# A four-layer convolution network on one core: sixth position of the first 3x3 convolution in filtered form, outer column sums and a normed residual moved to ScalarE and accumulating DMAs

## The chip, the cores and the metric

The kernel runs on one core of a Trainium2 chip. The metric is the device time of one execution in microseconds (us), as the median over several runs. The core has five engines with an instruction queue each, and every queue is worked off in order: PE (TensorE, matrix products; PEld is its weight load), DVE (VectorE), ACT (ScalarE), POOL (GpSimd) and SP (SyncE, which only issues transfers). Transfers issued by POOL go through one software queue (q0 in the profile), those of SP through a hardware queue (q1). Transfers that add to their destination (`accum_op=ALU.add`) are issued by POOL throughout this kernel.

## The reference, cut to what matters

Four layers, each `x = x + layer(groupnorm(x))`, on x of shape (4, 256, 56, 56) in float32. Layers 0 and 2 are involutions, layer 3 is a gate from a Fourier transform. The change lies in layer 1 alone, two 3x3 convolutions with batch norms and a residual:

```python
def _L1_conv_ref(x, w1, g1, b1, rm1, rv1, w2, g2, b2, rm2, rv2):
    h = _conv3x3(x, w1, stride=1)
    h = jax.nn.relu(_bn(h, g1, b1, rm1, rv1))
    h = _conv3x3(h, w2, stride=1)
    h = _bn(h, g2, b2, rm2, rv2)
    return jax.nn.relu(x + h)
# --- layer 1 ---
x = x + _L1_conv_ref(_gn(x), ...)
```

So with n = groupnorm(x) the layer's output is x + relu(n + conv branch): n enters the convolution and also stands as a residual inside the relu.

## The kernel before, in words

**Stages.** `involution_layer` runs for layer 0 (to about 509 us of the span), `conv_layer` for layer 1 (to about 1208 us), and `involution_layer` again for layer 2 with layer 3 folded into it.

**Tiling of layer 1.** The 256 channels are two blocks of 128 partitions. Each of the four images is cut into three chunks of rows; the first convolution's chunks have 20, 18 and 18 rows (`C1_ROWS`), the second's 16, 20 and 20 (`C2_ROWS`). That makes 12 chunks, numbered 0 to 11, for each convolution. They alternate: conv1(0), then conv1(1), conv2(0), conv1(2), conv2(1), ... conv1(11), conv2(10), conv2(11).

**Along the rows: six positions.** A row is taken in tiles of four outputs (`WT` = 14 tiles). `transform` turns the normed input into six planes v, and each 3x3 filter row becomes six values u; an output tile comes from six products, the "positions". They are worked in the order `KS` = 1, 2, 3, 4, 0, 5. Positions 1 to 4 are combined by sums and differences on DVE, 0 and 5 are added with factors at the end (L1523 to L1536).

**Between the rows: filtered or unfiltered.** An unfiltered position (`unfiltered`, L1449) takes the three filter rows one after the other: 12 matmuls with 128x128 weights over all the chunk's rows (252 columns for 18 rows, 280 for 20). A filtered position makes two output rows from four products of sums of neighbouring rows: 16 matmuls over half the columns (126 or 140). It needs `columns(i, k, half)` (L1425): half 0, the inner sums and differences (two DVE instructions, L1434 and L1435), and half 1, the outer difference of rows two apart (one DVE instruction over the whole chunk, L1432). It also needs combined weights (`column_weights`, `filter_weights`). In conv1(i) for i > 0, five positions (`K2`) are filtered and position 5 is unfiltered; conv1(0) and all of the second convolution are unfiltered.

**A filtered position, step by step** (L1483 to L1510). PE writes two pairs of PSUM banks: `inner`, from half 0, and then `outer`, from half 1. ACT copies the first inner bank to `h` (L1502), DVE makes h + second and h - second into the rows of the position's home tile (L1506, L1507), and then adds the outer pair (L1509). PSUM holds four such pairs, so PE starts the inner pair of a position when DVE has read the inner pair of two positions before.

**The second convolution's residual.** `residual(co)` (L1554) norms the input rows `xr` on ACT into the tile `res`, of which there is one buffer for both channel blocks; `joined(co)` (L1564) adds the convolution on DVE (L1568). `added` (L1580) is then run at once for block 0 and at the start of the next chunk for block 1: relu on ACT back into xr (L1582), a POOL transfer that adds the layer's input from DRAM (L1583), and a POOL transfer of the result to DRAM (L1584). In the last chunk DVE does this itself and SP stores.

**What sets the order.** `in_order` pins each engine's instructions to program order. `conv1` and `conv2` call the lists `after[0]` to `after[11]` at fixed places between their positions, and the loop at L1674 fills these lists: the next chunk's input (`phases` on ACT, `input1` and `input2` mostly on DVE), the statistics of finished rows, loads, and the column sums of the next conv1. `FIRST` lists the column sums prepared during the conv2 before, `LATER` those made inside conv1, as their buffers (five in rotation, `new_v2`) come free. In conv1(0) and conv1(1) the second convolution's weights are built by 18 accumulating transfers on POOL (`summed_weights`, L1281), each of which waits for an earlier one.

Of the kernel before, what the change touches and what calls it, by code (L numbers as in the profile page):

```python
# [16 lines left out]
P = 128  # L17
# [55 lines left out]
def net_kernel(  # L73
# [1109 lines left out]
    def conv_layer(xin, xout, st, ahead):  # L1183
        with ExitStack() as es:
# [13 lines left out]

            KS, K2 = (1, 2, 3, 4, 0, 5), (1, 2, 3, 4, 0)
            u1_sb = wpool.tile([P, NB, 3, WPOS, C], F32, name="u1_sb")  # L1200
# [5 lines left out]
            ux0_sb = room["rows"][:, n : n + NB * C].rearrange("p (c n) -> p c n", c=NB)  # L1206

            def between_weights(ci, k0, k1):

                return ux_sb[:, ci, k0 - 1 : k1 - 1, :] if k0 else ux0_sb[:, ci : ci + 1]  # L1210

# [13 lines left out]

            n_v2, n_h = [0], [0]

            def new_v2():
                n_v2[0] += 1
                at = (n_v2[0] - 1) % 5 * NY  # L1230
                return room["v2"][:, at : at + NY]

            def new_half():
                n_h[0] += 1
                return room["v2" if n_h[0] % 2 else "xr"][:, 5 * NY : 5 * NY + NY // 2]

# [62 lines left out]
            def column_weights(ci, k0, k1):  # L1299

                w0, w1, w2 = (u1_sb[:, ci, y, k0:k1, :] for y in range(3))
                x = between_weights(ci, k0, k1)
                s = y_tile(3 if k0 else 5)[:, : (k1 - k0) * C].rearrange("p (k n) -> p k n", n=C)
                tt(s, w0, w2, ALU.add)
                tt(x, s, w1, ALU.subtract)
                tt(w1, s, w1, ALU.add)
# [118 lines left out]
            def columns(i, k, half):  # L1425

                y0, y1, _, _ = rows1(i)
                m = (y1 - y0) // 2
                v = v_of[1, i][:, VP[k]].rearrange("p (r e c) t -> p e r (c t)", e=2, c=NB)
                t = v2_of[i, k, half] = new_v2().rearrange("p (e r n) -> p e r n", e=2, n=NB * WT)  # L1430
                if half:
                    tt(t[:, :, :m], v[:, :, :m], v[:, :, 1 : m + 1], ALU.subtract)  # L1432
                else:
                    tt(t[:, 0, :m], v[:, 1, :m], v[:, 0, 1 : m + 1], ALU.add)  # L1434
                    tt(t[:, 1, :m], v[:, 0, 1 : m + 1], v[:, 1, :m], ALU.subtract)  # L1435


            FIRST = [(K2[0], 0), (K2[0], 1), (K2[1], 0), (K2[1], 1), (K2[2], 0)]
            LATER = {0: [(K2[2], 1)], 1: [(K2[3], 0), (K2[3], 1)], 2: [(K2[4], 0), (K2[4], 1)]}

# [16 lines left out]
            def conv1(i, after, tail):  # L1457
# [4 lines left out]
                a, t, b, s, q = (y_tile(k)[:, : NB * n * WT] for k in (0, 1, 2, 5, 4))  # L1462
                first = y_tile(3)[:, : NB * n * WT] if i else q
                home = {1: first, 2: s, 3: t, 4: s, 0: s}

# [14 lines left out]
                for n_s, k in enumerate(KS):  # L1480
                    if k in K2 and i > 0:
# [7 lines left out]
                        for ps, bank, v2, e, u in work4:  # L1489
                            for co in range(NB):  # L1490
                                for ci in range(NB):
                                    nc.tensor.matmul(  # L1492
                                        ps[:, bank, co * m : (co + 1) * m],
                                        u[ci][:, co * P : (co + 1) * P],
                                        v2[:, e, : n // 2, ci * WT : (ci + 1) * WT],
                                        start=(ci == 0),
                                        stop=(ci == NB - 1),
                                    )
                        for late in LATER.get(n_s, ()):
                            columns(i, *late)  # L1500
                        h = new_half()[:, : NB * m]
                        nc.scalar.copy(h, inner[:, 0, : NB * m])  # L1502
                        o = home[k].rearrange("p (r e t) -> p e r t", e=2, t=WT)
                        rows_of = lambda x: x.rearrange("p (r t) -> p r t", t=WT)
                        m2 = rows_of(inner[:, 1, : NB * m])
                        tt(o[:, 0], rows_of(h), m2, ALU.add)  # L1506
                        tt(o[:, 1], rows_of(h), m2, ALU.subtract)  # L1507
                        run_all(after[2 * n_s])
# [31 lines left out]
            def conv2(i, after, sums, tail):  # L1540
# [9 lines left out]

                res = work.tile([P, CV_ROWS * W], F32, name="res", bufs=1)[:, : n * W]

                def residual(co):

                    x = xr_of[i, co][:, : n * W]
# [8 lines left out]
                def joined(co):  # L1564

                    y = room["h"][:, : 4 * NY].rearrange("p (j n) -> p j n", j=4)[:, :, co * m : (co + 1) * m]
                    rj = res.rearrange("p (j q) -> p j q", j=4)
                    stt(rj, y, s2_6[:, co : co + 1], rj, ALU.mult, ALU.add)  # L1568
# [17 lines left out]
                def stats(co, k):  # L1586
# [3 lines left out]
                    nc.vector.bn_stats(sums[co][:, at, :], xr_of[i, co][:, r0 * W : r1 * W])  # L1590

                for n_s, k in enumerate(KS[:4]):
                    pair = two_banks()
# [48 lines left out]
            order.append((2, n_chunks - 1))  # L1642
            late_v, late_x = None, []
            sums_of = {}
# [29 lines left out]
            for s, (conv, i) in enumerate(order):  # L1674
# [5 lines left out]
                after[0] += late_x  # L1680
                late_x.clear()
                if conv == 1:
                    after[0] += tail1
                    tail1 = []

                    if nxt[0] == 2:
                        j = nxt[1]
                        late_v = input2(j)
                        place(after, late_v, (1, 1, 3, 5, 8))
                        if j == 0:  # L1690
                            place(after, weights2, (0, 1, 2, 11))
                            for ci in range(NB):
                                after[0].append(lambda ci=ci: column_weights(ci, 0, 1))
                                after[1].append(lambda ci=ci: filter_weights(ci, 0, 1))
                        if i + 1 < n_chunks:
                            place(after, phases(i + 1), range(1, 10))
                            if i + 2 < n_chunks:
                                after[9].append(lambda i=i: load_rows(i + 2, xin))
                    else:
# [9 lines left out]
                        for n, (k, half) in enumerate(FIRST):  # L1709
                            after[(8, 8, 9, 9, 10)[n]].append(lambda k=k, half=half: columns(1, k, half))  # L1710
                        for ci in range(NB):
# [3 lines left out]
                else:  # L1715
# [10 lines left out]
                    if late_v is not None:  # L1726
                        place(after, late_v, (0, 0, 1, 1))
                        late_v = None
# [7 lines left out]
                    if nxt is not None and nxt[0] == 1:  # L1736
                        j = nxt[1]
                        place(after, input1(j), (0, 0, 1, 1, 2, 3, 4, 5, 6))
                        for n, (k, half) in enumerate(FIRST):
                            after[(4, 5, 6, 7, 8)[n]].append(lambda j=j, k=k, half=half: columns(j, k, half))  # L1740
                    elif nxt is not None:
# [92 lines left out]
```

## Time and profile before

| what | us |
|---|---|
| runs, median of 3 (lowest to highest) | 1760.48 (1759.03 to 1763.52) |
| the profiled execution | 1761.49 |
| span of the profile | 1759.7 |
| PE busy in the span | 1687.6 (96%) |
| DVE / ACT / POOL busy | 1338.6 / 912.6 / 417.5 |
| layer 1, first to last matmul of L1453 and L1492 | 521.8 to 1207.4 |

Each float32 matmul stands twice in the records, so 2136 records of L1453 are 1068 matmuls. A row of the timeline gives the start, the length, the engine, the line and operation, and in brackets the idle time before it and what ended it; consecutive instructions of one kind are merged. A row of the windows gives a stretch, its length, and the busy time of PE, PEld, DVE, ACT and POOL in it (with the number of instructions), the granted TensorE clock, the busy share of the 16 DMA engines, and GB/s.

### The profile page before, as it was taken

What the parts mean: (1) busy time and instruction counts of PE and PEld (TensorE: products, weight loads), DVE (VectorE), ACT (ScalarE), POOL (GpSimd) and SP (SyncE); (2) the same over time, 40 slices, a digit from 0 to 9 for tenths busy, and PEclk for the clock granted to TensorE, in tenths of its full rate; (3) what the DMA queues carried; (4) which work ended last, traced back from release to release, by engine and by line L of the source; (5) the groups of instructions that cost most, each with busy time, mean ns of one, the idle gap of its engine ahead of it and who ended that gap; (6) DMA issues with size and microseconds to landing.
All of it is one profiled execution on the core that took longest, in us unless ns stands there. A gap on an engine that the chain in (4) does not pass through costs nothing.

```text
span 1759.7 us, 55922 instructions
## 1 busy us (share of the span) xinstructions
PE 1687.6 (96%) x24216; PEld 1494.0 (85%) x24216; DVE 1338.6 (76%) x2469; ACT 912.6 (52%) x1948; POOL 417.5 (24%) x609
## 2 busy tenths in 40 slices
PE   6999999999999999999999999998999999989998
PEld 4988988889978988898899889986988888878886
DVE  2777787777769888888889888955777678767775
ACT  2655556456546434443344334324767567557564
POOL 2223322333234000000000000001000563562572
PEclk9999999999989999999999999999999999999996
DMA  2355444533669323321333122243444666664653
GB/s 87 126 165 160 134 152 155 185 107 119 200 208 246 84 84 80 104 74 44 96 87 90 53 78 63 53 147 114 145 141 149 204 216 200 201 203 153 191 155 114
DMA packets 79876, 236.12 MB, mean 134 GB/s; under 512 B 13494, under 2 KB 29631, under 8 KB 75919
## 3 DMA queue, kind: packets, MB, share of 16 engines
q1 hardware_dynamic: 57438, 163.33, 29.4%
q0 software_dynamic: 21152, 67.95, 14.8%
q8 instruction: 191, 3.13, 0.7%
q10 hardware_dynamic: 1040, 1.26, 0.3%
q14 instruction: 55, 0.44, 0.1%
HBM read 95.07 MB, written 49.15 MB: 82 GB/s over the span
## 4 chain that ended last, share of the span: by engine, by line
PE 71%; DVE 13%; DMA 5%; ACT 4%; issue 3%; SPq 1%; POOL 1%; ACTq 0%; DVEq 0%; POOLq 0%
PE mm L1453 24%; PE ps L635 14%; PE ps L593 14%; PE mm L1492 9%; DVE kt L611 5%; PE ps L407 3%; DMA xw<-xw 3%; DVE un L655 3%; PE ps L469 2%; DMA u_sb<-in_wc_dram 1%; DVE st L1105 1%; ACT hp L488 1%; ACT xw L419 1%; PE ps L718 1%; PE ps L947 1%
## 5 line engine op out<-in xcount | busy, mean ns | idle before, releaser
L1453 PE MATMUL mm<-v,u_sb 128*128 128x280 f32 (+2 forms) x2136 | 475.6, 384 | 0.0
L1453 PEld LDWEIGHTS mm<-v,u_sb 128*128 128x128 f32 x2136 | 402.8, 189 | 67.8 <-issue 0.4
L635 PE MATMUL ps<-kt,xw 126*32 126x48 f32 (+1 forms) x12544 | 381.9, 236 | 23.0 <-issue 14.9
L635 PEld LDWEIGHTS ps<-kt,xw 126*32 126x32 f32 (+1 forms) x12544 | 344.3, 122 | 68.7 <-issue 47.3
L593 PE MATMUL ps<-hp,z_sb 64*126 64x133 f32 x6144 | 382.6, 279 | 8.1 <-DVE kt L611 4.9
L593 PEld LDWEIGHTS ps<-hp,z_sb 64*126 64x126 f32 x6144 | 363.6, 185 | 23.5 <-DVE kt L611 6.6
L611 DVE TENSOR_TENSOR kt<-ps,zb_sb 126x798 f32<-126x798 f32 x352 | 333.0, 981 | 58.8 <-PE ps L593 47.5
L604 ACT ACTIVATE kt<-ps,zb_sb 126x133 f32<-126x133 f32 x960 | 280.3, 441 | 105.9 <-PE ps L593 105.9
L655 DVE SCALAR_TENSOR_TENSOR un<-ps,s,un 128x240 f32<-128x240 f32 x224 | 102.5, 458 | 89.0 <-ACT un L650 84.9
L1492 PE MATMUL mm<-xs,u_sb 128*128 128x126 f32 (+1 forms) x1320 | 163.0, 277 | 7.0 <-DVE hp L1507 3.3
L1492 PEld LDWEIGHTS mm<-xs,u_sb 128*128 128x128 f32 x1320 | 156.3, 191 | 9.1 <-ACT ph L1361 4.0
L655 DVE SCALAR_TENSOR_TENSOR un<-ps,par_sb,un 128x240 f32<-128x240 f32 x224 | 97.8, 457 | 83.9 <-ACT un L648 79.9
L419 ACT COPY xw<-ps 126x896 f32<-126x896 f32 x112 | 101.3, 906 | 46.8 <-DMA xw<-xw 23.6
L660 POOL TENSOR_TENSOR xs<-un,xs 128x240 f32<-128x240 f32 x112 | 72.2, 665 | 218.2 <-DVE un L655 218.1
L407 PE MATMUL ps<-ident_sb,strip_sb 128*126 128x128 f32 x784 | 113.9, 286 | 9.7 <-issue 4.3
L1583 POOL DMA_DIRECT2D xs<-x x22 | 19.6, 889 | 430.6 <-ACT xs L1582 430.6
L648 ACT ACTIVATE un<-ps,par_sb 128x240 f32<-128x240 f32 x112 | 50.2, 448 | 120.8 <-PE ps L635 115.7
L650 ACT ACTIVATE un<-ps,bn_t,s 128x240 f32<-128x240 f32 x112 | 60.0, 537 | 91.3 <-PE ps L635 85.7
L1582 ACT ACTIVATE xs<-res 128x1120 f32<-128x1120 f32 (+1 forms) x22 | 46.4, 2107 | 117.0 <-DVE res L1568 117.0
L150 POOL TENSOR_TENSOR norm_sb<-norm_sb,mhalf 128x1 f32<-128x1 f32 x32 | 19.1, 598 | 368.7 <-DVE norm_sb L149 368.7
L407 PEld LDWEIGHTS ps<-ident_sb,strip_sb 128*126 128x126 f32 x784 | 86.2, 143 | 21.5 <-issue 5.8
L1361 ACT ACTIVATE ph<-xs,norm_sb 128x294 f32<-128x294 f32 (+2 forms) x96 | 78.8, 864 | 8.4 <-DMA xs<-x 6.7
(265 smaller groups left out, 1900.0 us busy)
## 6 DMA issues: line engine op xcount, KB each, us to landing
xw<-xw SPq DMA_DIRECT2D x224, 252.0 KB
xw<-xw SPq DMA_DIRECT2D x224, 126.0 KB
xs<-x SPq DMA_DIRECT2D x24, 560.0 KB
x<-xs POOLq DMA_DIRECT2D x8, 1568.0 KB, 8.1
xs<-x SPq DMA_DIRECT2D x8, 1568.0 KB
xs<-in_x_dram SPq DMA_DIRECT2D x6, 1568.0 KB
x<-xs SPq DMA_DIRECT2D x6, 1568.0 KB
gx<-x POOLq DMA_DIRECT2D x42, 224.0 KB, 5.1
```

Of the source, the lines that this page charges most:

```text
L407: nc.tensor.transpose(ps[:Q, k * P : (k + 1) * P], flat[:, k * Q : (k + 1) * Q], ident_sb)
L419: nc.scalar.copy(xw[:, :NSB, :], ps[:Q, : NSB * P].rearrange("q (n c) -> q n c", n=NSB))
L593: nc.tensor.matmul(ps[:Q, i, k * NT : (k + 1) * NT], z_sb[i * R : (i + 1) * R, cb * GB // 2 + gp, z0 : z0 + Q], hp[i * R : (i + 1) * R, py ...
L604: nc.scalar.activation(kt[:, g0 + i, pb, :, k], ps[:Q, i, k * NT : (k + 1) * NT], AF.Identity, bias=zb_sb[:, cb * GB + g0 + i, p0 + k : p0 ...
L611: nc.vector.tensor_tensor(kt[:, g0 : g0 + 2, pb], ps[:Q, :, : PB * NT].rearrange("q i (k t) -> q i t k", k=PB), zb_sb[:, cb * GB + g0 : cb ...
L635: nc.tensor.matmul(v[m * j : m * j + m, i, :, k * TP : (k + 1) * TP], xw[:, window(ty), m * j : m * j + m], kt[:, ng * j : ng * j + ng, :, ...
L650: nc.scalar.activation(part, o[0], AF.Identity, bias=bn["t4"][:, cb : cb + 1], scale=bn["s4"][ng][:, 0, cb : cb + 1])
L655: nc.vector.scalar_tensor_tensor(part, o[e], s, part, ALU.mult, ALU.add)
L660: nc.gpsimd.tensor_tensor(dst, u, dst, ALU.add)
L1361: nc.scalar.activation(dst, xr[:, j], AF.Identity, bias=t, scale=s)
L1453: nc.tensor.matmul(ps, *position(u, v, ci, dy, k, co, n), start=(j == 0), stop=(j == NB * 3 - 1))
L1492: nc.tensor.matmul(ps[:, bank, co * m : (co + 1) * m], u[ci][:, co * P : (co + 1) * P], v2[:, e, : n // 2, ci * WT : (ci + 1) * WT], start ...
```

## The change

All of it is in layer 1.

1. Position 5 of the first convolution is filtered too (`K2` = all six). Its combined weights need a new tile `ux5_sb` and a piece of the tile `hp`; they are made during conv1(1).
2. `columns` with half 1 is no longer a DVE subtraction. ACT writes minus the later rows into the buffer, and a POOL transfer with accumulation adds the earlier rows. The buffers are now three for each half. Half 0 stays on DVE.
3. In a filtered position ACT copies the first inner bank straight into the home tile, and DVE subtracts and adds in place; the tile `h` is gone. The home tiles are assigned anew.
4. In conv2 of chunks 0 to 9 (`summed`), ACT norms xr in place (`scaled`, in `after[6]` and `after[8]`); `joined` scales the convolution on ACT into `res` and a POOL transfer adds `res` to xr. In the next chunk ACT does the relu in place (`after[4]`, `after[8]`), a POOL transfer adds the layer's input (one list later), and SP stores (`after[7]`, `after[11]`). Chunks 10 and 11 stay as they were.
5. The places of `input1`, `input2` and the column sums in the lists are shifted by one or two.

```diff
-            KS, K2 = (1, 2, 3, 4, 0, 5), (1, 2, 3, 4, 0)
+            KS = K2 = (1, 2, 3, 4, 0, 5)
...
+                if k0 == 5:
+                    return ux5_sb if ci else room["h"][:, 5 * NY : 5 * NY + C].rearrange("p (k n) -> p k n", k=1)
...
+            def new_v2(half):
+                n_v2[half] += 1
+                at = (n_v2[half] - 1) % 3
+                if half:
+                    return [room["v2"][:, at * NY : (at + 1) * NY]]
...
             def columns(i, k, half):
                 if half:
-                    tt(t[:, :, :m], v[:, :, :m], v[:, :, 1 : m + 1], ALU.subtract)
+                    (t,) = new_v2(1)
+                    v = v.rearrange("p r t -> p (r t)")
+                    at = slice(0, n * NB * WT)
+                    nc.scalar.mul(t[:, at], v[:, 2 * NB * WT : (n + 2) * NB * WT], -1.0)
+                    nc.gpsimd.dma_start(t[:, at], v[:, at], accum_op=ALU.add)
...
-            FIRST = [(K2[0], 0), (K2[0], 1), (K2[1], 0), (K2[1], 1), (K2[2], 0)]
-            LATER = {0: [(K2[2], 1)], 1: [(K2[3], 0), (K2[3], 1)], 2: [(K2[4], 0), (K2[4], 1)]}
+            FIRST = [(k, half) for k in K2[:3] for half in range(2)]
+            LATER = {n: [(K2[n + 3], half) for half in range(2)] for n in range(len(K2) - 3)}
...
-                home = {1: first, 2: s, 3: t, 4: s, 0: s}
+                first = s if i else q
+                home = {1: s, 2: q, 3: t, 4: s, 0: y_tile(3)[:, : NB * n * WT], 5: s}
...
+                        nc.scalar.copy(o[:, 0], m1)
                         for late in LATER.get(n_s, ()):
                             columns(i, *late)
-                        h = new_half()[:, : NB * m]
-                        nc.scalar.copy(h, inner[:, 0, : NB * m])
-                        tt(o[:, 0], rows_of(h), m2, ALU.add)
-                        tt(o[:, 1], rows_of(h), m2, ALU.subtract)
+                        tt(o[:, 1], o[:, 0], m2, ALU.subtract)
+                        tt(o[:, 0], o[:, 0], m2, ALU.add)
...
+                summed = i < n_chunks - 2
+                def scaled(co):
+                    x = xr_of[i, co][:, : n * W]
+                    s, t = rstd[:, co : co + 1], shift2[:, co : co + 1]
+                    nc.scalar.activation(x, x, AF.Identity, bias=t, scale=s)
...
                 def joined(co):
+                    if summed:
+                        x, at = xr_of[i, co][:, : n * W], slice(y0 * W, y1 * W)
+                        nc.scalar.mul(res.rearrange("p (q j) -> p j q", j=4), y, s2_6[:, co : co + 1])
+                        nc.gpsimd.dma_start(x, res, accum_op=ALU.add)
+                        k = 4 * (co + 1)
+                        late_r[k].append(lambda: nc.scalar.activation(x, x, AF.Relu))
+                        late_r[k + 1].append(lambda: nc.gpsimd.dma_start(x, xin[bb][co][:, at], accum_op=ALU.add))
+                        late_r[k + 3].append(lambda: nc.sync.dma_start(xout[bb][co][:, at], x))
+                        return
...
-                        place(after, late_v, (1, 1, 3, 5, 8))
+                        place(after, late_v, (1, 3, 5, 8))
...
+                                after[2].append(lambda ci=ci: column_weights(ci, 5, 6))
+                                after[3].append(lambda ci=ci: filter_weights(ci, 5, 6))
...
-                            after[(8, 8, 9, 9, 10)[n]].append(lambda k=k, half=half: columns(1, k, half))
+                            after[(8, 8, 9, 9, 10, 10)[n]].append(lambda k=k, half=half: columns(1, k, half))
...
-                        place(after, late_v, (0, 0, 1, 1))
+                        place(after, late_v, (0, 0, 0, 1, 1))
...
-                        place(after, input1(j), (0, 0, 1, 1, 2, 3, 4, 5, 6))
+                        place(after, input1(j), (1, 1, 2, 2, 3, 3, 4, 4, 5))
...
-                            after[(4, 5, 6, 7, 8)[n]].append(lambda j=j, k=k, half=half: columns(j, k, half))
+                            after[(5, 5, 6, 6, 7, 7)[n]].append(lambda j=j, k=k, half=half: columns(j, k, half))
```

## The prediction

> **What bounds the kernel now.** I read the page's shares first, then the chain that ended last inside layer 1, the waits of PE, and then windows and timelines of single chunks. PE is busy for 1687.6 of 1759.7 us. In layer 1 the chain is PE nearly throughout:
>
> ```profile
> by line: PE mm L1453 60.7%; PE mm L1492 23.5%; DMA u_sb<-in_wc_dram 3.7%; ACT xs L1582 1.3%; PE mm L274 1.3%; DVE res L1568 0.8%; ACT res L1556 0.7%; DVE v L1392 0.6%; PE mm L1660 0.6%; DVE xs L1432 0.5%; issue 0.5%; SPq L1271 0.5%; POOL u_
> ...
> 553.25 8.31 DMA u_sb<-in_wc_dram
> ...
> 668.21 19.07 PE mm L1492 x160
> ...
> 744.76 32.34 PE mm L1453 x168
> 777.11 17.86 PE mm L1492 x160
> 794.97 5.10 PE mm L1453 x24
> ```
>
> The reader is to see the prices: 80 filtered matmuls (160 records) take 17.86 us at 126 columns, 223 ns each, and 19.07 us at 140 columns, 238 ns each. The unfiltered position 5 takes 5.10 us (24 records). Second, only the start of layer 1 has a transfer in its chain, that of the second convolution's weights.
>
> PE waits little once layer 1 is under way. Windows of two conv1 chunks, first matmul to last, the first with 18 rows and the second with 20:
>
> ```profile
> core 0: us, PE busy (x) PEld busy (x) DVE busy (x) ACT busy (x) POOL busy (x), PEclk, DMA share, GB/s
> ...
> 726.70:749.90 23.20, 23.20 (x187) 22.60 (x186) 20.72 (x39) 14.43 (x21) 2.45 (x4) 1.00 0.58 153
> ...
> 834.68:862.00 27.32, 25.50 (x186) 23.87 (x186) 22.50 (x40) 15.28 (x23) 3.63 (x6) 1.00 0.52 124
> ```
>
> conv1(4) has no hole in PE. conv1(6), and conv1(9) like it, lose 2.6 us: their 160 records take 21.7 us (834.68 to 856.37) where conv1(3) took 19.07. So making DVE lighter is worth about 5 us here, no more; PE's own work is the prize, and the danger is a new wait. Where one could arise is at the seam from conv2 to conv1:
>
> ```profile
> 723.74 2.24 ACT L1582 ACTIVATE xs<-res 128x1120 f32<-128x1120 f32 x1 [10.77 <-DVE res L1568]
> ...
> 726.28 0.86 POOL L1583 DMA_DIRECT2D xs<-x  x1 [44.57 <-ACT xs L1582]
> ...
> 726.74 1.05 PE L1492 MATMUL mm<-xs,u_sb 128*128 128x126 f32 x8
> ...
> 728.72 0.37 ACT L1502 COPY xs<-mm 128x252 f32<-128x252 f32 x1 [0.28 <-PE mm L1492]
> ...
> 732.16 0.56 POOL L1584 DMA_DIRECT2D x<-xs  x1 [5.03 <-DMA xs<-x]
> ```
>
> The accumulating transfer of 560 KB was issued at 726.28 and what waits for it went on at 732.16, 5.9 us later. Today nothing but the store waits for that. The copy of the first position (L1502) runs 2 us after PE's start.
>
> **What the skill says.** The Trainium skill, "DMA: Bandwidth & Descriptors", section "Anatomy of one DMA — SWDGE (gpsimd) path", gives about 2.0 us fixed plus bytes over 436 GB/s, so 3.3 us for 560 KB. This trace is slower for accumulating transfers, by the summary of line L1583 and by a window in which only that transfer runs, with all 16 engines full at 206 GB/s:
>
> ```profile
> DMA to landing us min/median/max: 5.1/5.7/6.9
> ```
> ```profile
> 729.20:730.20 1.00, 1.00 (x12) 1.00 (x11) 1.00 (x2) 0.30 (x1) 0.00 (x0) 1.00 1.04 206
> ```
>
> The forecast goes by the trace. The same page ("Two DMAs through the same engine are not ordered") says that descriptors of one queue on an engine start in order. I use that: a small transfer behind a large one on POOL's queue begins when the large one has been read.
>
> **The change part by part.** The sum is made against the profiled execution (1761.49 us), which is 1.0 above the median.
>
> *PE, removed and added.* Eleven chunks lose 12 matmuls and gain 16. At 18 rows: 5.05 us (5.10 alone; 4.99 when 27.35 for 144 records of 224 columns is taken from 32.34) less 16 x 223 ns = 3.57, a gain of 1.48. At 20 rows: 24 x 236.6 ns per record (conv2's 34.07 us for 144) = 5.68 less 16 x 238 ns = 3.81, a gain of 1.87. Leaving out conv1(1), that is 7 x 1.48 + 3 x 1.87 = 16.0 us.
>
> *DVE.* Per chunk it loses five outer differences (0.68 each) and gains one position (0.82 for the inner sums, 0.82 and 0.68 to combine); in ten chunks it loses two joins of 1.39 or 1.15. That is about 3.5 us per pair of chunks. It hides behind PE, except in conv1(6) and conv1(9), whose 2.6 us each were a DVE backlog: their first combination began at 838.00, behind a join that ended at 837.4. That is 5.2 us back. The new combined weights for position 5 (six DVE operations of 0.43, six of ACT at 0.41) fall into conv1(1), where PE waits anyway.
>
> *ACT.* It gains six multiplications of about 0.62 (the 512-element row of L1297) per conv1. In conv2 three operations replace two: the contiguous norm and relu (no row has 1120 contiguous elements; between 0.83, the 768-element row of L1291, and 2.26; I take 1.1) and the strided scaling (2.26, as L1582). The sum stays near 9 us, and ACT is busy for 285 of the 705 us from 505 to 1210, so the amount costs nothing. Its order does.
>
> *The seam.* `res` has one buffer. The scaling for block 1 must wait until the transfer for block 0 has read `res`, and ACT stands meanwhile: behind it in ACT's queue are the copy of the first position and the multiplication for position 4's outer columns. In the times of the timeline above: block 0's result is ready at 722.2 (L1623's end), scaling to 724.5, POOL issues at 724.8 (same 0.3 as above), lands 5.9 later at 730.7. Block 1's scaling runs to 733.0, the copy to 733.4, and two DVE combinations (0.35 + 0.41) to 734.2. PE's third position needs those PSUM banks at 726.7 + 2 x 3.57 = 733.85: a wait of 0.4. The multiplication ends at 734.05 and its transfer issues at 734.3. It follows block 1's 560 KB, issued 733.3, landing 739.2 and read by about 738.3. Its 252 KB take 1.25 us at 206 GB/s and 0.9 to be signalled: 740.45. The fourth position's outer half wants it at 726.7 + 3 x 3.57 + 1.79 + 0.4 = 739.6: another 0.85. So 1.2 us in conv1(4), (7), (10). After a 16-row conv2 (448 KB, 5.3 us, scaling 1.84) the same sum gives 0.5 in conv1(2), (5), (8), (11); with 20 rows, whose positions last 3.81, 0.5 in conv1(3), (6), (9). Together 3 x 1.2 + 7 x 0.5 = 7.1 us. The later outer columns (issued near 736 and 739) have over 2 us of room. The relus and the adding of the layer's input come after these in ACT's and POOL's queues and have a whole chunk. SP's stores sit ahead of loads that are due much later.
>
> *The start.* In conv1(1), POOL's queue interleaves the six new column transfers with the 18 weight transfers, and the last of them stands behind the eighteenth. Those weights land 8.8 us after issue (7.5 to 11.4); the last was issued at 571.75, so 580.8. Queue q0 is saturated there, with 16 engines busy and 209 GB/s in 560:580. Six times 252 KB at about 195 GB/s add 6 x 1.3 = 7.9 us: the last columns land near 588.7, the eight matmuls after them take 1.8, and conv2(0) starts at about 590.5 instead of 583.8. I take 6.5 us lost. From above it is 10, if POOL also stands while ACT waits for PE to free a column buffer; from below 1, if gaps in the queue take the transfers up.
>
> *Sum.* -16.0 - 5.2 + 7.1 + 6.5 = -7.6: 1753.9 for the profiled execution, 1753 as a median (16.0 + 5.2 + 1.48 would be the most to win).
>
> **The rivals.**
>
> *A, the forecast:* as above, 1753; with the ends of the start's cost and 0.3 us per seam either way, 1745 to 1760.
>
> *B, slower: the seam decides.* Every microsecond that the accumulating transfer from SBUF takes beyond 5.9 is added to ACT's stall, and from there to PE at ten seams. The gain is 7.6 us, so it is gone at 0.76 us more, 6.7 us, which lies inside the 5.1 to 6.9 of L1583. The weights' 8.8 us would give +29: about 1782; 8 us gives 1774. For it: ACT's margin is below half a microsecond, and the SBUF-to-SBUF transfers of the trace (u_sb from u_sb) showed a median of 9.1. Against it: those were three deep in the queue and in 1 KB pieces, while at the seam nothing else is in flight, with pieces of 3.5 to 4.4 KB.
>
> *C, nothing to measure:* the start costs 10 and the seams 1.2 each (12 instead of 7.1). Then -21.2 + 22: 1761.
>
> *D, more:* the SBUF source lands faster than DRAM, by 1 us. The seam waits vanish (7.1) and the start costs 4: 1743.
>
> That the change does not do what it says is not likely: in the changed program's order PE has 16 matmuls of 126 columns for position 5.
>
> **How the numbers follow.** A 0.47, B 0.28, C 0.13, D 0.12. About 0.3% (5.3 us) is what a measurement of this kernel can tell from no change, so faster means below 1755.2 and slower above 1765.8. A is faster in 0.42 of its 0.47 and D wholly: 0.54. The rest of A and C: 0.18. B: 0.28. The range from 1743 to 1775 leaves out the upper half of B and the lower half of D, 2 in 10; A's own is 1745 to 1760.
>
> **What would show it.** Right: position 5 with records of 126 and 140 columns, 3.57 or 3.81 us per position; conv1(4) near 22.6 us from its first to its last matmul, where five filtered positions and the unfiltered one took 22.9; ACT's second scaling starting about 4 us after PE's first conv1 matmul, waiting for a transfer; PE waits of about a microsecond at the third and fourth position of conv1; conv2(0) starting near 590. Wrong: landings of 7 us or more for the transfer out of `res` (B), conv1(1) ending after 594 (C), or no PE waits at the seams (D). I would also be wrong if DVE, which gets its first combination 2.7 us later than now, carried that delay through the whole of conv1.

## The result: 1785.3 us, slower by 1.3%

The changed kernel takes 1785.31 us (median of 4 runs, 1780.02 to 1787.53) where the kernel before takes 1761.28 (4 runs, 1759.03 to 1763.52): a ratio of 1.0131, 95% interval 1.0109 to 1.0153. The forecast was 1753 us, with a range of 1743 to 1775. The profiled execution took 1784.47 us, 23.0 more than that of before. Layer 1, from its first to its last large matmul, went from 685.2 to 706.8 us; this holds nearly all of the difference, and the rest of the program is the same in both.

To see where, I split layer 1 into three groups by the starts of the chunks. A "round" is one conv1 chunk with the conv2 chunk that follows it; "pair" stays the word for two PSUM banks.

| group | before | after | difference | forecast |
|---|---|---|---|---|
| the start: conv1(0), conv1(1), conv2(0) | 88.9 | 101.2 | +12.3 | +6.5 |
| the rounds of conv1(2), (3), (4), (7), (10) | 266.2 | 258.6 | -7.7 | -3.2 |
| the rounds of conv1(5), (6), (8), (9), (11), and the last conv2 | 330.1 | 347.0 | +17.0 | -10.9 |

The forecast's column is its own sum, sorted the same way: in the second group 4 x 1.48 + 1.87 won and 4.6 lost at seams, in the third 3 x 1.48 + 2 x 1.87 + 5.2 won and 2.5 lost. So one group did better than forecast, the start cost twice as much, and the third group went the wrong way by 28 us.

**The group that worked.** The same two chunks as in the prediction, conv1(4) and conv1(6), each in a window from its first matmul to the first of the next chunk.

```profile
core 0: us, PE busy (x) PEld busy (x) DVE busy (x) ACT busy (x) POOL busy (x), PEclk, DMA share, GB/s
734.00:755.45 21.45, 21.45 (x193) 21.40 (x193) 16.80 (x35) 15.56 (x24) 5.20 (x6) 1.00 0.72 125
844.84:875.28 30.44, 26.23 (x195) 25.87 (x195) 19.78 (x38) 16.62 (x26) 6.61 (x8) 0.89 0.57 110
```

conv1(4) now has six filtered positions in 21.45 us with no hole in PE: 6 x 3.57 = 21.4, as priced. conv1(6), which should take 6 x 3.81 = 22.9, takes 30.4, with 4.2 us of holes and a clock that was not full. The seam of conv1(4), in the timeline:

```profile
732.15 0.86 POOL L1591 DMA_DIRECT2D xs<-res  x1 [10.29 <-ACT res L1590]
734.05 1.05 PE L1505 MATMUL mm<-xs,u_sb 128*128 128x126 f32 x8
...
737.01 2.33 ACT L1590 ACTIVATE res<-hp,s 128x1120 f32<-128x1120 f32 x1 [5.15 <-DMA xs<-res]
...
739.14 0.41 ACT L1514 COPY xs<-mm 128x252 f32<-128x252 f32 x1
739.41 2.84 PE L1505 MATMUL mm<-xs,u_sb 128*128 128x126 f32 x24
```

ScalarE (ACT) does stand for the transfer out of `res`, and the copy of the first position (L1514) does come 3 us after PE had finished the inner pair that it reads (736.0). But what waits for the transfer goes on 4.9 us after the issue (732.15 to 737.01), not 5.9. The summary of line L1591, 448 and 560 KB together, has a median landing of 4.7 us, where L1583 before had 5.7:

```profile
DMA to landing us min/median/max: 4.2/4.7/4.9
```

DVE has therefore freed the first pair of PSUM banks at 740.5, and PE needs it at 741.2. No wait follows here.

**The group that failed.** The same seam in conv1(6):

```profile
843.50 0.86 POOL L1591 DMA_DIRECT2D xs<-res  x1 [11.08 <-issue]
844.47 0.50 PE L229 MATMUL mm<-d,gavg_sb 128*128 128x1 f32 x4
...
844.84 1.20 PE L1505 MATMUL mm<-xs,u_sb 128*128 128x140 f32 x8
...
846.83 2.07 PE L1505 MATMUL mm<-xs,u_sb 128*128 128x140 f32 x16
...
848.63 2.26 ACT L1590 ACTIVATE res<-hp,s 128x1120 f32<-128x1120 f32 x1 [6.34 <-DMA xs<-res]
850.70 0.43 ACT L1514 COPY xs<-mm 128x280 f32<-128x280 f32 x1
...
851.64 0.45 DVE L1518 TENSOR_TENSOR xs<-xs,mm 128x280 f32<-128x280 f32 x1
...
852.23 2.20 PE L1505 MATMUL mm<-xs,u_sb 128*128 128x140 f32 x8 [3.33 <-DVE xs L1518]
```

Here PE stops after one position, not two, and waits for the same copy. The reason is in the row of L229. It is a group norm's matmul: one column wide, but `one_bank` takes a whole pair of PSUM banks for it, and there are four pairs. The norm of an image is advanced by a list `slow`, one step in `after[5]` and one in `after[11]` of each chunk. A matmul issued in `after[11]` is read by DVE in `after[5]` of the next chunk; there are two channel blocks, so two of the four pairs are gone meanwhile. The groups of the two matmul lines, L218 and L229, and of their readers, L221 and L149, around conv1(6) (durations in ns, then the first and last start in us):

```profile
L218 PE MATMUL mm<-mv,gavg_sb x4: 170/250/271, 805.7 to 806.6; 128*128 128x1 f32 x4
...
L221 DVE COPY gm<-mm x2: 151/151/151, 829.5 to 830.1; 128x1 f32<-128x1 f32 x2
...
L229 PE MATMUL mm<-d,gavg_sb x4: 166/250/250, 844.5 to 844.7; 128*128 128x1 f32 x4
...
L149 DVE TENSOR_SCALAR norm_sb<-mm x2: 147/150/152, 864.4 to 864.4; 128x1 f32<-128x1 f32 x2
```

Two pairs are held from 806 to 830 and from 844.5 to 864.4, that is, over the end of conv1(5), the start of conv2(4) and the start of conv1(6). The same happens for the next images at conv1(8), (9) and conv1(11). A filtered position uses two pairs; with two left, the next position starts only when DVE has read the one just finished. From 600 us on, waits for such a pair are most of what PE waits for in layer 1; the two largest groups are

```profile
PE mm L1505 <- DVE xs L1518: 9.1, 5, 3.3
PE mm L1466 <- DVE xs L1518: 5.8, 3, 1.9
```

(us in total, times, longest). L1518 is the DVE instruction that frees an inner pair. Not all of these are waits with pairs held: the 1.1 and 1.7 us at the third position of conv1(5) and (8) come at a time when all four pairs are in use by the convolution alone.

**The clock.** The matmuls behind the hole of conv1(6) are slow: 2.20 us for eight records that take 1.19 elsewhere. In all fourteen profiles of this case the granted clock (third column from the end) changes only at the borders of a grid of 3.41 us, so here are four windows on that grid:

```profile
847.66:851.07 3.41, 1.24 (x11) 1.02 (x9) 0.00 (x0) 2.44 (x3) 0.00 (x0) 1.00 0.02 2
851.07:854.48 3.41, 2.25 (x10) 2.28 (x11) 2.29 (x5) 1.74 (x4) 1.75 (x2) 0.50 0.60 113
854.48:857.90 3.42, 3.42 (x16) 3.42 (x16) 1.76 (x4) 0.39 (x1) 0.00 (x0) 0.50 0.75 139
857.90:861.31 3.41, 3.41 (x31) 3.41 (x30) 2.15 (x4) 2.22 (x4) 0.86 (x1) 1.00 0.02 5
```

PE was idle for 2.2 us of the first window (3.41 less 1.24). TensorE then had half its clock for two windows, of which 5.7 us were matmuls. At half speed these cost about half of that, 2.8 us, beside the 3.3 us of the hole itself. The same happened behind three other holes, ahead of conv2(4), (7) and (10). By the same estimate the halved clock cost 9.2 us from 600 us on, and all of it in the third group. Two more halved windows lie in the start.

**The start.** conv1(1) waits four times for column transfers, 10.4 us in all, the last two times for 3.56 and 3.88 us:

```profile
581.27 4.54 PE L1505 MATMUL mm<-xs,u_sb 128*128 128x126 f32 x24 [3.56 <-DMA xs<-v]
590.59 2.78 PE L1505 MATMUL mm<-xs,u_sb 128*128 128x126 f32 x16 [3.88 <-DMA xs<-v]
```

### The profile page after: what moved, and what is told of

It reads as the page before. It is cut to its first block, busy times and chain, and to the rows that moved or that the text cites. A ratio compares the mean times of both kernels' runs of the same rounds, so it can differ in the third digit from the quotient of the medians.

```text
span 1782.7 us, 56439 instructions
## 1 busy us (share of the span) xinstructions
PE 1679.6 (94%) x24304; PEld 1492.4 (84%) x24304; DVE 1311.0 (74%) x2455; ACT 950.7 (53%) x2051; POOL 481.3 (27%) x675
## 3 DMA queue, kind: packets, MB, share of 16 engines
q1 hardware_dynamic: 60318, 173.89, 30.4%
## 4 chain that ended last, share of the span: by engine, by line
PE 53%; issue 17%; DVE 13%; DMA 8%; ACT 4%; POOL 4%; SPq 1%; ACTq 0%; POOLq 0%; DVEq 0%
PE ps L593 14%; PE ps L635 13%; PE mm L1466 12%; DVE kt L611 5%; PE mm L1505 5%; DMA xw<-xw 4%; DVE un L655 3%; PE ps L407 3%; DMA u_sb<-in_wc_dram 2%; PE ps L469 2%; DMA xs<-res 1%; POOL xs L1441 1%; DVE st L1105 1%; DMA xs<-v 1%; ACT hp L488 1%
## 5 line engine op out<-in xcount | busy, mean ns | idle before, releaser
L1466 PE MATMUL mm<-v,u_sb 128*128 128x280 f32 (+1 forms) x1872 | 424.2, 389 | 5.8 <-DVE xs L1518 5.8
L1466 PEld LDWEIGHTS mm<-v,u_sb 128*128 128x128 f32 x1872 | 357.7, 192 | 68.8 <-issue 6.5
L1505 PE MATMUL mm<-xs,u_sb 128*128 128x126 f32 (+1 forms) x1584 | 199.6, 281 | 24.3 <-DMA xs<-v 10.4
L1505 PEld LDWEIGHTS mm<-xs,u_sb 128*128 128x128 f32 x1584 | 191.4, 195 | 27.1 <-ACT v L1373 10.0
L1441 POOL DMA_DIRECT2D xs<-v x66 | 63.2, 998 | 255.7 <-ACT xs L1440 255.2
L1590 ACT ACTIVATE res<-hp,s 128x1120 f32<-128x1120 f32 (+1 forms) x20 | 43.0, 2151 | 106.3 <-DVE hp L1656 55.2
```

The source lines that it names most:

```text
L1441: nc.gpsimd.dma_start(t[:, at], v[:, at], accum_op=ALU.add)
L1466: nc.tensor.matmul(ps, *position(u, v, ci, dy, k, co, n), start=(j == 0), stop=(j == NB * 3 - 1))
L1505: nc.tensor.matmul(ps[:, bank, co * m : (co + 1) * m], u[ci][:, co * P : (co + 1) * P], v2[e][:, : n // 2, ci * WT : (ci + 1) * WT], start ...
```

## The experiments

Theory P: the norm's matmuls hold PSUM pairs, and that costs the third group. Its rivals are S (ScalarE standing at the seam; some expectations call it R), D (the load of DVE) and the transfers of the start (Q). In the expectation of two_res5 alone, S stands for the start. All times below are medians; the last three columns are the groups of layer 1 against before, from one profile each.

| run | us | ratio to before (95%) | start | five good rounds | other rounds |
|---|---|---|---|---|---|
| after | 1785.3 | 1.0131 [1.0109, 1.0153] | +12.3 | -7.7 | +17.0 |
| norm_short | 1757.6 | 0.9969 [0.9954, 0.9985] | +12.1 | -7.6 | -5.0 |
| seam_only | 1762.5 | 0.9993 [0.9975, 1.0011] | +12.7 | -8.0 | -6.0 |
| start_dve | 1767.6 | 1.0017 [1.0002, 1.0032] | +1.9 | -8.0 | +7.8 |
| no_sum | 1799.4 | 1.0201 [1.0170, 1.0232] | +13.3 | +13.6 | +5.2 |
| cols_dve | 1790.0 | 1.0146 [1.0126, 1.0165] | +4.0 | -3.4 | +26.8 |
| before_short | 1755.2 | 0.9966 [0.9947, 0.9986] | +0.2 | 0.0 | -5.1 |
| short_start | 1742.2 | 0.9890 [0.9861, 0.9918] | +2.8 | -7.8 | -6.9 |
| filter_only | 1748.9 | 0.9933 [0.9912, 0.9953] | +2.0 | -8.0 | -0.8 |
| cols_dve_short | 1767.4 | 1.0004 [0.9989, 1.0018] | +2.8 | -1.8 | +7.8 |
| two_res | 1738.4 | 0.9875 [0.9844, 0.9906] | +4.3 | -8.0 | -13.4 |
| two_res_cols_dve | 1747.6 | 0.9906 [0.9877, 0.9934] | +3.8 | -8.0 | -3.9 |
| two_res5 | 1740.1 | 0.9856 [0.9832, 0.9879] | -0.2 | -8.0 | -13.4 |

The kernel before had medians of 1761 to 1766 us beside these, so the ratios compare better than the times.

### norm_short: the norm gives its pairs back within a chunk

```diff
-                for g in slow:
-                    after[5].append(step(g))
-                    after[11].append(step(g))
+                for g in slow[:1]:
+                    after[5].append(step(g))
+                    after[11].append(step(g))
+                for g in slow[1:]:
+                    for k in (5,) if conv == 1 else (2, 3, 6, 7, 9):
+                        after[k].append(step(g))
```

> The changed kernel, but the group norm's small matmuls of finished images (L218 and L229, two PSUM pairs at a time) are made and read in the middle of one second-convolution chunk (lists 2, 3, 6, 7, 9), so that no pair is held across a seam. Theory P (two of four PSUM pairs are held by these matmuls from the end of conv1(5), (8), (11) into conv2, and from the end of conv2(4), (7) into conv1(6), (9); PE then stalls on DVE or ACT and the TensorE clock is halved for some 4 us afterwards): conv1(6) falls from 30.6 to about 23 us and conv1(9) from 26.7 to 23, the holes of 2.9 to 3.3 us before conv2(4), (7), (10) go with the slow stretch behind them: 22 to 27 us less, about 1760. Rival R (ACT standing before the second scaling, because res has one buffer, is what stalls PE at the seams whatever the pairs): no more than 3 us less, 1782 to 1788.

1757.6 us: 28 us come back, 22 of them in layer 1 and all of these in the third group (+17.0 to -5.0). The rest lies in the program behind layer 1, which no run changed and which took between 546 and 559 us in the fourteen profiles. The norm's matmuls and their readers now fall between the seams (conv1(6) begins at 840.47):

```profile
813.48 0.50 PE L218 MATMUL mm<-mv,gavg_sb 128*128 128x1 f32 x4
...
821.40 0.15 DVE L221 COPY gm<-mm 128x1 f32<-128x1 f32 x1
...
825.24 0.50 PE L229 MATMUL mm<-d,gavg_sb 128*128 128x1 f32 x4
...
832.98 0.22 DVE L149 TENSOR_SCALAR norm_sb<-mm 128x1 f32<-128x1 f32 x2
```

No halved clock is left between 600 us and the end of layer 1, so some 9 of the 22 us are the clock. Theory P holds as far as this: without held pairs the loss is gone.

### start_dve: conv1(1)'s outer columns on DVE

```diff
-                    nc.scalar.mul(t[:, at], v[:, 2 * NB * WT : (n + 2) * NB * WT], -1.0)
-                    nc.gpsimd.dma_start(t[:, at], v[:, at], accum_op=ALU.add)
+                    if i == 1:
+                        tt(t[:, at], v[:, at], v[:, 2 * NB * WT : (n + 2) * NB * WT], ALU.subtract)
+                    else:
+                        nc.scalar.mul(t[:, at], v[:, 2 * NB * WT : (n + 2) * NB * WT], -1.0)
+                        nc.gpsimd.dma_start(t[:, at], v[:, at], accum_op=ALU.add)
```

> The changed kernel, but the outer column sums of conv1(1) alone are made by one DVE subtraction each, as in the kernel before; those of conv1(2) to (11) stay with ACT and transfers. Theory Q (the six transfers stand among the 18 saturating weight transfers in POOL's queue): conv1(1), from its first matmul to conv2(0)'s first, falls from 39.0 us to 26 to 28, total about 1774. Rival (conv1(1) is late because of ACT's and DVE's work on the new weights): it stays above 35, total 1782 or more.

The start's group falls from +12.3 to +1.9: the transfers of the columns, between those of the weights, cost 10.4 us. The rest of the gain was not expected: +17.0 to +7.8 in the third group, whose instructions are those of after. There the hole of conv1(6) was 2.2 us and not 3.3, because POOL issued the first transfer earlier (2.2 us before PE began conv1(6), not 1.3), and the clock stayed full. Two other holes of this profile, ahead of conv2(4) and conv2(7), are alike in length and in what ends them, but not in what follows:

```profile
798.65 34.20 PE L1469 MATMUL mm<-v,u_sb 128*128 128x280 f32 x144 [1.92 <-DVE xs L1521]
...
968.41 35.69 PE L1469 MATMUL mm<-v,u_sb 128*128 128x280 f32 x144 [1.92 <-DVE xs L1521]
```
```profile
793.95:797.36 3.41, 2.29 (x21) 2.12 (x19) 3.31 (x7) 2.09 (x5) 0.00 (x0) 1.00 0.94 226
797.36:800.78 3.42, 2.13 (x9) 1.78 (x10) 3.21 (x7) 1.10 (x2) 0.00 (x0) 1.00 1.03 402
...
964.62:968.03 3.41, 1.38 (x12) 1.21 (x11) 3.31 (x7) 1.69 (x5) 0.00 (x0) 1.00 1.04 287
968.03:971.44 3.41, 3.03 (x7) 2.28 (x8) 3.24 (x5) 0.59 (x2) 0.00 (x0) 0.50 0.95 387
```

Each of these holes is 2.9 us long, with the norm's four records inside (so 1.92 us in the bracket). The windows lie on the clock's grid. The first hole was split by a border, 1.1 us of idle PE on one side and 1.3 on the other, and the clock stayed full. The second left 2.0 us idle in one window; half the clock followed, and 144 matmul records took 1.5 us longer. This holds throughout. In layer 1 of all fourteen profiles, 27 windows at full clock had at least 1.92 us without a matmul record, and each was followed by half the clock; the other 2748 had at most 1.86, and none was. So a hole of 3.45 us in conv1(5) of cols_dve_short cost no clock (1.68 and 1.77 us on the two sides of a border), and one of 2.35 us in conv1(6) of cols_dve did. The profiles began anywhere from 0.2 to 2.8 us behind a border of the grid, though the program's first part is the same in all. So whether a hole of 2 to 3.5 us costs clock is a matter of chance for the kernel, and the third group can vary by several us between runs.

### before_short: the same norm edit on the kernel before

The edit is that of norm_short, made in the kernel before.

> The kernel before with the group norm's matmuls placed as in norm_short. Theory P: the 2.6 us that conv1(6) and conv1(9) lose there are the held PSUM pairs too, not a backlog of DVE as the prediction said: both go from 21.7 to 19.1 us for their filtered positions, 5 us less, about 1756. If it was DVE's backlog: unchanged.

The filtered positions of conv1(6) and conv1(9) take 19.1 us and not 21.7, and PE is busy throughout, as in conv1(6):

```profile
837.32:856.39 19.07, 19.07 (x162) 19.07 (x161) 17.29 (x31) 12.09 (x16) 2.45 (x4) 1.00 0.61 150
```

The 2.6 us each that the prediction called a DVE backlog were held pairs too. The kernel before also paid for them, but only while DVE was late.

### no_sum: the residual back on DVE and POOL

```diff
-                summed = i < n_chunks - 2
+                summed = False
```

> The changed kernel, but the second convolution's residual as in the kernel before in all chunks (no scaling into res, no third transfer). Rival R: all seams clear, 15 to 20 us less, about 1767. Theory P: conv1(6) and (9) go back to about 27 us as in the kernel before (5 us less in all with their clock), while the holes before conv2(4), (7), (10) stay or grow by a microsecond, since DVE has the joins again: 1777 to 1787.

Neither value came out: 1799.4 us, worse than after. The third group is better, but the good rounds lose 21 us. From 600 us on PE waits for column transfers in six places, 17.2 us in all, where the changed kernel has no such wait. The two timelines, of POOL and of PE, show the cause at conv1(4):

```profile
743.43 0.87 POOL L1613 DMA_DIRECT2D xs<-x  x1 [12.19 <-ACT xs L1612]
749.65 0.56 POOL L1614 DMA_DIRECT2D x<-xs  x1 [5.34 <-DMA xs<-x]
750.20 0.90 POOL L1441 DMA_DIRECT2D xs<-v  x1
...
758.75 0.56 POOL L1614 DMA_DIRECT2D x<-xs  x1 [6.77 <-DMA xs<-x]
759.30 1.79 POOL L1441 DMA_DIRECT2D xs<-v  x2
```
```profile
764.15 1.02 PE L1505 MATMUL mm<-xs,u_sb 128*128 128x126 f32 x7 [4.01 <-DMA xs<-v]
```

The old residual's store (L1614) is issued by POOL and stands there until the adding transfer has landed; the column transfers (L1441) stand behind it. By these rows parts 2 and 4 of the change depend on each other: the columns can be on POOL because the store went to SP. A run of no_sum with the store on SP, which would show it, was not made.

### cols_dve: all outer columns on DVE

As start_dve, for every chunk.

> The changed kernel, but all outer column sums are made by DVE, as in the kernel before. It tells what the move of these sums to ACT and transfers is worth beside its cost at the start. Theory Q: the start gives back 11 us as in start_dve. Theory P: DVE is later at the end of each conv1 by about 2 us (three subtractions of 0.68), so the holes before conv2(4), (7), (10) grow by 1 to 3 us each: 1775 to 1782. If DVE has room in conv1 after all, the same as start_dve, 1774.

1790.0 us, above both values expected and 22 more than start_dve, most of it in the third group (+26.8 against +7.8). The columns on DVE make it later, and the pairs are still held. How much of this is DVE's load, and how much ScalarE standing later because DVE delivers later, this run does not tell; cols_dve_short and two_res_cols_dve below do, without held pairs.

### short_start: norm_short and start_dve together

> The changed kernel with both edits of norm_short and start_dve. If the two causes are separate, their gains add up but for the share of start_dve's that came from the seams: conv1(1) near 29 us and conv1(6), (9) near 23 to 24: 1745 to 1750, below the kernel before. If they are two views of one cause (PE's stalls as such), no more than 3 us below norm_short's 1757.6.

1742.2 us, better than before by 1.1% and a little under the 1745 to 1750 expected. The two gains nearly add up: 28 us from the norm, 15 more from the start, which alone gave 18.

### filter_only: position 5 filtered, all columns and the residual on DVE

The edits are those of norm_short, cols_dve and no_sum.

> The sixth position filtered alone: the changed kernel with the norm's matmuls as in norm_short, but all outer column sums on DVE and the residual as in the kernel before. PE's own work is the same as in the changed kernel. If DVE keeps up, 16 us below before_short, 1740. Theory D (with six filtered positions DVE has no room in conv1: some 3.5 us more per pair of chunks than in the changed kernel, in a conv1 that is 1.5 us shorter): PE waits for DVE in every conv1, which then takes 23 to 25 us instead of 21.4: 1755 to 1770.

1748.9 us, less than the 1755 to 1770 expected of a DVE that is too heavily laden. But DVE does not quite keep up either: the 16 us that PE is spared against before_short come out as some 6 (a ratio of 0.9933 against 0.9966), and PE waits up to 1.7 us in conv1(5), (8) and (11) and inside conv2(4) and (7). What the change takes off DVE is worth 7 us more in short_start and about 10 in two_res.

### cols_dve_short: only the residual moved, the columns on DVE

The edits are those of norm_short and cols_dve.

> The changed kernel with the norm's PSUM pairs given back within a chunk, and all outer column differences made by DVE; the residual stays with ScalarE and the transfers. It stands between short_start (1742.2, columns on ScalarE and POOL) and filter_only (1748.9, both on DVE). If DVE's load is what costs filter_only its 7 us, the time lies between the two, 1744 to 1747, and conv1(5), (8), (11) between 23.0 and 24.4 us. If the residual alone matters, it is 1742 like short_start; if the columns alone matter, 1749 like filter_only.

A clear miss: 1767.4 us. Moving the residual off DVE makes layer 1 slower than in filter_only, 694.0 us against 678.4. At conv1(8):

```profile
951.34 0.86 POOL L1594 DMA_DIRECT2D xs<-res  x1 [32.84 <-ACT res L1593]
...
956.29 1.87 ACT L1593 ACTIVATE res<-hp,s 128x896 f32<-128x896 f32 x1 [5.24 <-DMA xs<-res]
957.96 0.41 ACT L1517 COPY xs<-mm 128x252 f32<-128x252 f32 x1
...
958.85 0.42 DVE L1521 TENSOR_TENSOR xs<-xs,mm 128x252 f32<-128x252 f32 x1
...
959.41 2.05 PE L1508 MATMUL mm<-xs,u_sb 128*128 128x126 f32 x8 [3.76 <-DVE xs L1521]
```

The columns delay DVE's end of conv2, so block 0's transfer is issued 3.0 us after PE's first conv1 matmul (948.34). ScalarE stands until 956.29, and the copy comes after PE's third position was due. The hole is 3.8 us, and the next eight records take 2.05 us, at half clock. Here all four pairs are free. This is the seam of the prediction, deciding.

### two_res: a second place for the scaled result

On short_start: block 0's scaled result goes into planes 1 and 2 of `v_of[2, i]`, which are free by then, in two pieces; block 1's stays in `res`. ScalarE has no transfer to wait for.

```diff
-                        nc.scalar.mul(res.rearrange("p (q j) -> p j q", j=4), y, s2_6[:, co : co + 1])
-                        nc.gpsimd.dma_start(x, res, accum_op=ALU.add)
+                        if co == 0:
+                            into = v[:, 1:3, : n * NB].rearrange("p k r t -> p k (r t)")
+                            for h in range(2):
+                                nc.scalar.mul(
+                                    into[:, h].rearrange("p (q j) -> p j q", j=4),
+                                    y[:, :, h * m // 2 : (h + 1) * m // 2],
+                                    s2_6[:, co : co + 1],
+                                )
+                            nc.gpsimd.dma_start(x.rearrange("p (h e) -> p h e", h=2), into, accum_op=ALU.add)
+                        else:
...
```

> short_start, and block 0's scaled result goes into two planes of the second convolution's input that PE has finished with, so the scaling of block 1 no longer waits for block 0's transfer. Theory R, as far as it is left: the stalls of 1 to 2 us at the third position of conv1(5), (8), (11) and small ones in (3), (6), (9) go: 4 to 8 us below short_start, about 1741. If PE's remaining stalls come from DVE alone: within 2 us of short_start.

1738.4 us. From conv1(2) on every conv1 takes what its matmuls take, conv1(6) for one:

```profile
832.90:855.80 22.90, 22.90 (x193) 22.86 (x192) 18.80 (x35) 16.73 (x25) 5.20 (x6) 1.00 0.74 134
```

The third group stands at -13.4 us, the 8.2 + 5.2 of the prediction without its seams. That it agrees to the tenth is partly luck: the conv1 chunks won 14.7 us, and the conv2 chunks, where the norm's matmuls now stand, lost 1.4. The step from short_start to two_res is within the error as a time; it is read from layer 1 (673.3 to 668.2 us) and from the holes that are gone.

### seam_only: the same on the changed kernel, with held pairs

> The changed kernel with only the second place for block 0's scaled result: the norm keeps its PSUM pairs, the start is as changed. Theory P (the held pairs alone cost the 28 us): the gain is what the second place brought without held pairs, about 4 us, so about 1781, with conv1(6), (9) near 30 and 26 us. Theory P x S (held pairs cost that much because the copy of the first position stands behind ScalarE's wait for res, and the pair it would free is one of two): conv1(6), (9) fall to 22.9 to 24 us, while the holes ahead of conv2(4), (7), (10), which wait for DVE and not for ScalarE, stay at about 3 us; the time is 1764 to 1774. Theory S (the seam alone): 1750 to 1756.

1762.5 us, just under the range of "P x S", with conv1(6), (9) at 24.8 and 24.7 us, just over it. So the held pairs alone are not the cause either: with ScalarE free, the first position's copy comes at 847.30, 2.95 us after PE began conv1(6) at 844.35 (5.86 us in the changed kernel), and two pairs nearly suffice. The waits for DVE ahead of conv2(4), (7), (10) fell too, from 1.9 us to between 0.8 and 1.6, which I had not expected. In the third group norm_short and seam_only each take away 22 to 23 us of what after lost, and two_res, with both (and the start's edit), 30. The loss needs both causes at once, and taking either away is enough for most of it.

### two_res_cols_dve: cols_dve_short with the second place

> cols_dve_short with the second place for block 0's scaled result, as in two_res. In cols_dve_short PE waits four times up to 3.8 us for the first combination, which stands behind ScalarE's copy, which stands behind the second scaling, which waits for the transfer out of res. Theory S (ScalarE standing at the seam, made late by DVE's columns, costs the 25 us between cols_dve_short and short_start): with two places ScalarE never stands, conv1(5), (8), (11) fall from 26.3 to 27.9 us to 21.4 to 22.5, and the time to 1740 to 1747. Theory D (DVE has too much work beside the residual's transfers, wherever ScalarE stands): conv1(5), (8), (11) stay above 24.5 us and the time above 1755.

1747.6 us against the 1767.4 of cols_dve_short, and in layer 1 677.2 against 694.0: these 17 us were ScalarE standing, with the halved clock behind it. conv1(5), (8), (11) take 24.1, 23.3 and 22.7 us, between the two theories: some of D is true, since with the columns on DVE the third group keeps 9.5 us that two_res does not have.

### two_res5: position 5 not filtered in conv1(1)

On two_res; the position's combined weights are made during conv2(0).

> As two_res, but position 5 stays unfiltered in conv1(1), and its combined weights are made during conv2(0). Theory S (conv1(1) of the start is held up by DVE and by the weights' transfers, so that everything added there is paid): conv1(1), from its first matmul to the unfiltered stretch after it, falls from 31.1 to about 27.5 us and the time by 2 to 4 us, to about 1735. Rival (conv1(1) waits for the weights of the second convolution's six positions, whatever is done beside them): within 1 us of two_res, 1737 to 1739.

The start's group falls by 4.5 us, to the value of before, as its theory S said. The time is equal to two_res within the error (ratios 0.9856 and 0.9875, with overlapping intervals). These two are the best versions, 22 to 25 us faster than before.

## Why the prediction was wrong, step by step

- **PE's removed and added work** (16.0 us): right. The five good rounds won 7.7 where 7.8 were worked out without seams, and two_res has every conv1 from conv1(2) on at the length of its matmuls.
- **DVE, "5.2 us back" in conv1(6) and (9)**: the size was right and the cause wrong. before_short wins 5.1 us in the third group without touching DVE's load. The prediction looked at DVE's first combination at 838.00 and at the join before it, and stopped there; the wait of PE for a pair that should have been free was not asked about.
- **The seam** (7.1 us): this is where the prediction failed. Its chain from the transfer over ScalarE's copy and DVE to PE was right, as cols_dve_short and two_res show. The step that failed is "PE's third position needs those PSUM banks", which counts four pairs everywhere, as the description of a filtered position does. With two pairs held it is the second position, 3.8 us earlier, and a wait of a fraction of a microsecond becomes a hole of 3.3 us in conv1(6) and 2.2 in conv1(9); holes of 2.9 to 3.3 us ahead of conv2(4), (7), (10) were not in the sum at all. The landing was mis-sized in the other direction (4.9 instead of 5.9), so that the seams with four pairs cost nothing at conv1(2), (4), (7), (10) and 1.2 to 2.2 us at conv1(5), (8), (11) (norm_short), where block 0's transfer is issued later: 0.7 us after conv1(5) began, but 1.3 us before conv1(2) did. The second wait of the seam, of the fourth position for its column transfer (0.85 us), never showed: from 600 us on no PE wait of the changed kernel ends with a column transfer.
- **The start** (6.5, at most 10): mis-sized. It cost 12.3 us, of which start_dve gives back 10.4; leaving position 5 unfiltered there takes the rest (two_res5, -0.2 after +4.3 in two_res). One pair is held in conv1(1) too, from 554.3 to 574.5 us, and likewise in the kernel before; what that costs was not tested. The transfers were worked out as bytes behind the last weights; their landing was 8.2 to 14.8 us in 500:600 since they stood between the weights for all of the chunk, and PE waited four times rather than once.
- **Not in the sum**: the clock. A seam was priced at its length; a hole can cost 1.5 to 3 us more, 9.2 us in all in the third group. The Trainium skill, "TensorE: Matmul & The Clock Gate" (Part 1, "What's actually happening"), has this: half clock after an idle window of about 3.4 us that runs freely. The profiles agree on the window and its free run, the grid of 3.41 us. They differ on the idle: a window need not be empty, since 1.92 us without a matmul were enough here, and a hole of 3.45 us across a border was not.
- **Rival B**, slower because of the seam, came nearest in time (1774 to 1782), but by a transfer slower than 5.9 us. The transfer was faster, so the nearness is luck. B did not ask either how many pairs PE really has at each seam.

## What to carry to other kernels

Before pricing a delay by the depth of a buffer, list everyone who takes from that pool and for how long: here two results one column wide held half of the pairs for 20 us, which cost 5 us in the kernel before, and 22 once the copies came late. When an engine gets a new wait, ask what stands behind it at each place of the schedule, not at a typical one; the same seam cost nothing in five chunks and up to 7.5 us in the others. Two causes that are needed together look, in single experiments, as if each were the whole, so run both and their combination.

## What was not expected of the hardware

- The accumulating transfers from SBUF to SBUF (448 and 560 KB) landed in 4.7 us (median; 4.9 at most); those from DRAM in the kernel before in 5.7.
- In layer 1 of these fourteen profiles it was not the length of a hole that decided the clock but the idle time within one stretch of a fixed 3.41 us grid: 1.92 us or more were followed by a granted clock of 0.50, 1.86 or less by 1.00. A halved clock became full again after a stretch with at most 0.38 us idle, and stayed halved after one with 0.65 or more. Every halving that began in layer 1 lasted for 3.4 or 6.8 us.
